# Three background chains in a row instead of overlapping, earlier weight preparation, and a one-pass spread of the softmax maximum

## The chip, the cores and the metric

The kernel runs on one core of one Trainium2 chip. The metric is the device time of one launch in microseconds (us). Five engines work side by side, each with its own queue of instructions that it executes in order: TensorE (PE in the profile, its weight loads PEld), VectorE (DVE), ScalarE (ACT), GpSimd (POOL) and SyncE (SP, which here issues all DMAs).

## The reference

The input `x` has 8 batches of 64 tokens with 512 channels, the context has 8 batches of 1601 rows with 512 channels. Six residual blocks follow one another:

```python
x = x + xattn(layernorm(x), ctx, Wq, bq, Wkv, bkv, Wo, bo)   # 32 query heads, 8 key/value heads of 128
x = x + mamba(layernorm(x), ...)                             # projection, conv of 4, silu, selective scan, gate
x = x + ffn(layernorm(x), ternarize(weight), bias)
x = x + softmax(layernorm(x) @ ctx.T) @ ctx
x = x + causal_attention(layernorm(x), wq, wk, wv, wo)       # 32 heads of 16
x = x + octonion_ffn(layernorm(x), w_gate, w_up, w_down)     # ternary weights
```

The scan of the second block keeps, for each of 1024 channels, 16 states: `state = state * exp(dt * A) + dt * u * B`, `y = sum(state * C)`, over the 64 tokens of a batch.

## The kernel before

**Main work.** `x_all` (L527) computes the first block. It runs over 64 units, one for each batch b and key/value head i (unit 8b + i). A unit has six steps: keys (`x_k`, L354), values (`x_v`, L319), scores (`x_s`, L369) with a copy to SBUF and a running maximum, then for the unit before it `x_max`, `x_spread`, `x_exp`, `x_av` and `x_o`, and `x_wo` (L496) for the output projection of two batches. Keys, values and scores are computed in three float32r products (high and low parts), the rest in float32.

**The maximum.** `x_max` (L397) transposes the maxima into PSUM (L403), and DVE reduces them to one negated column `mc` (L405). `x_spread` (L408) spreads that column over all partitions with a matmul against the identity, `m_ps` (L412), once for each half of 128 queries; `x_exp` adds it to the scores (L426) before the exponential. Column and identity are float32. TensorE executes a float32 matmul here as two instructions, a float32r matmul or a transpose as one.

**Background work.** Two kinds of generators run beside the units. `prep` (L616) splits and ternarizes the weights of the later blocks and writes them to DRAM. `chain` (L779) takes a group of two batches through blocks two to six: `mamba`, `ffn`, `xattn1`, `attn1`, `ffn1`. There are four groups, so chains 0 to 3. Chains 0, 1 and 2 are started when the main work has finished batches 1, 3 and 5. Chain 3 starts after the last unit, in another form ("tail"), with more PSUM and SBUF buffers.

**Pace.** Each `yield` of a generator reports a cost. `run` (L1303) keeps a clock `now` that advances by one for each batch of main work (236 cost units), and `advance` (L1331) draws from each background generator until it has got its share: its total cost (`CHAIN_COST` 377, `PREP_COST` 168) times the elapsed part of its span (`SPAN`, and `PREP_END` for `prep`). With the spans of before, 3.1 batches for chains 0 and 1, chain 1 starts before chain 0 has ended, and chain 2 before chain 1.

**Order.** That pace gives only the order in which the program is written. A scheduler then fixes each engine's order. The instructions of background work on DVE, ACT and POOL are pinned (class `Late`, L55): they keep the written order among themselves on their engine, so what is written later can't overtake. In the profile they all have line L65, whatever they do; on TensorE the background work has its own lines.

**The scan.** `scan` (L895) is called 32 times for each of chains 0 to 2: four blocks of states (`sh`), eight channel groups (`c`) each. A call does four exponentials on ACT into a tile `da`, a memset and a product `h = B * du` on POOL (called M1 in what follows), the scan on DVE, a product with C on POOL (M2), a reduction on DVE, and an addition into `u` on POOL (for `sh` 0 instead another product on POOL at its start and an operation on DVE). `da` and `h` are two of the five buffers named `a2`; the tile `bc` with B and C has one buffer and is loaded anew for each `sh`. The four steps of a call are followed by a `yield 1` each, so 128 of a chain's 377 cost units belong to the scan. After the scans come the gates (16 matmuls at L819 for each half), and `mamba_out` with 24 matmuls at L774, L776 and L777.

**The end.** When the last unit is done, `run` closes the pools of the main work and of `mamba`'s tiles (`ca`), and chain 3 gets its buffers from that memory:

```python
if last:
    self.pinning = False
    xctx.close()
    actx.close()
    self.pc = ctx.enter_context(tc.tile_pool(name="pt", bufs=3, space=PSUM))
    self.ca = self.cp = self.tp = ctx.enter_context(tc.tile_pool(name="tp", bufs=2))
```

Of the kernel before, what the change touches and what calls it, by code (L numbers as in the profile page):

```python
# [9 lines left out]
FR = mybir.dt.float32r  # L10
# [6 lines left out]
P = 128  # L17
# [61 lines left out]
class Kernel:  # L79
# [67 lines left out]
    def consts(self):  # L147
        nc, i = self.nc, self.i
        c = self.ctx.enter_context(self.tc.tile_pool(name="const", bufs=1))
        self.c = c  # L150
        self.ident = c.tile([P, P], FP, name="ident")
        make_identity(nc, self.ident)
        self.eps5 = c.tile([P, 1], FP, name="eps5")
        nc.gpsimd.memset(self.eps5, 1e-5)
        self.ones = c.tile([P, P], FP, name="ones")
        nc.gpsimd.memset(self.ones, 1.0)
        self.eps6 = c.tile([P, 1], FP, name="eps6")
        nc.gpsimd.memset(self.eps6, 1e-6)

        def ld(name, shape):  # L160
            t = c.tile(shape, FP, name="c_" + name)
            nc.sync.dma_start(out=t, in_=i[name])
            return t

        self.bq = ld("bq", [P, 32])
        self.bk = ld("bk", [P, NKV])
        self.bv = ld("bv", [P, NKV])
# [229 lines left out]
    def x_max(self, b, i):  # L397

        nc = self.nc
        m = self.mf.pop((b, i))  # L400
        ps = self.px.tile([P, 2, 256], FP, name=self.nm("m_ps"), tag="m", bufs=MB)
        for h in range(2):
            nc.tensor.transpose(ps[:, 0, h * P : (h + 1) * P], m[:, 0, h * P : (h + 1) * P], self.ident)  # L403
        col = self.sb("mc", [P, 2], pool=self.xp, bufs=2)
        nc.vector.tensor_reduce(col, ps[:, 0].rearrange("p (h k) -> p h k", k=P), AX.X, ALU.max, negate=True)  # L405
        self.mm[(b, i)] = (ps, col)

    def x_spread(self, b, i):  # L408

        ps, col = self.mm[(b, i)]  # L410
        for h in range(2):
            self.nc.tensor.matmul(  # L412
                ps[:, 1, h * P : (h + 1) * P], lhsT=col[:, h : h + 1].to_broadcast([P, P]), rhs=self.ident, start=True, stop=True
            )

    def x_exp(self, b, i, n):
# [390 lines left out]
    def mamba(self, gi, x, xo):  # L807
        nc, i = self.nc, self.i
# [36 lines left out]
        ps = self.acc()  # L845
# [20 lines left out]
        for h in range(2):  # L866
            ps = self.acc()
# [27 lines left out]
        def scan(c, sh, bc):  # L895
            da = self.sb(self.td, [P, HS, 2, T])
            for s in range(HS):
                k = sh * HS + s
                nc.scalar.activation(da[:, s], dt[:, c], AF.Exp, scale=self.A[:, c, k : k + 1])
            nc.gpsimd.memset(da[:, :, :, 0:1], 0.0)  # L900
            du = dus[:, c]
            if sh == 0:
                nc.gpsimd.tensor_tensor(du, dt[:, c], u[:, c], ALU.mult)
            h = self.sb(self.ts, [P, HS, 2, T])
            nc.gpsimd.tensor_tensor(h, bc[:, 0], du[:, None].to_broadcast([P, HS, 2, T]), ALU.mult)

            yield 1
            hf, df = h.rearrange("p s b t -> p (s b t)"), da.rearrange("p s b t -> p (s b t)")
            nc.vector.tensor_tensor_scan(hf, df, hf, 0.0, ALU.mult, ALU.add)
            yield 1  # L910
            nc.gpsimd.tensor_tensor(h, h, bc[:, 1], ALU.mult)
            yield 1
            y = da[:, 0]
            nc.vector.tensor_reduce(y.rearrange("p b t -> p (b t)"), h.rearrange("p s b t -> p (b t) s"), AX.X, ALU.add)
            if sh == 0:
                nc.vector.scalar_tensor_tensor(u[:, c], u[:, c], self.Dp[:, c : c + 1], y, ALU.mult, ALU.add)
            else:
                nc.gpsimd.tensor_tensor(u[:, c], u[:, c], y, ALU.add)
            yield 1

        wps = None
        if tail:
# [18 lines left out]
            for c in range(NCH):  # L941
                du = self.sb("du", [P, 2, T])
                nc.gpsimd.tensor_tensor(du, dt[:, c], u[:, c], ALU.mult)
                for k0 in range(0, NST, CS):
# [6 lines left out]
                    h = h8[:, o : o + CS]  # L951
# [14 lines left out]
        else:  # L966
            for sh in range(nh):
                bc = bcast(sh)
                for c in range(NCH):
                    yield from scan(c, sh, bc)  # L970
# [332 lines left out]
    def run(self):  # L1303
        nc, tc, ctx = self.nc, self.tc, self.ctx
        nc.scalar.preload_act_table_set("natural_log_exp_and_others")
        self.setup(bufs=BUFS, accb=2, hs=4, tail=False, ahead=1, **TAGS)
        self.pc = ctx.enter_context(tc.tile_pool(name="pc", bufs=2, space=PSUM))
        xctx = ctx.enter_context(ExitStack())
        self.px = xctx.enter_context(tc.tile_pool(name="px", bufs=2, space=PSUM))
        self.consts()  # L1310
        self.scratch()
        self.xw = ctx.enter_context(tc.tile_pool(name="xw", bufs=2))
        self.xp = xctx.enter_context(tc.tile_pool(name="xp", bufs=2))
        qctx = ctx.enter_context(ExitStack())
        self.q_ln(qctx.enter_context(tc.tile_pool(name="qp", bufs=2, side="right")))
        B = self.B
        sizes = GROUPS.get(B) or [1] * B
        groups, k = [], 0
        for m in sizes:
            groups.append(list(range(k, k + m)))  # L1320
            k += m
        self.place = {b: (k * T, len(g) * T) for g in groups for k, b in enumerate(g)}
        side, self.tp = [], None

        def start(gen, now, cost, end):
            env = {k: getattr(self, k) for k in ENV}
            if not self.tail:
                env["nc"] = Side(self, PINNED)
            side.append({"gen": gen, "cost": cost, "got": 0.0, "t0": now, "end": end, "env": env})

        def advance(now):  # L1331
            base = {k: getattr(self, k, None) for k in ENV}
            for c in list(side):
                self.setup(**c["env"])
                goal = c["cost"] * min(1.0, (now - c["t0"]) / max(c["end"] - c["t0"], 1e-9))
                if now >= c["end"]:
                    goal = 1e9
                while c["got"] < goal:
                    try:
                        c["got"] += next(c["gen"])  # L1340
                    except StopIteration:
                        if PRINT_COST:
                            print("side", c["got"])
                        side.remove(c)
                        break
            self.setup(**base)

        gi, now, xdone = 0, 0.0, 0.0
        for cost, fin in self.x_all(list(range(B))):
            xdone += cost  # L1350
            if not self.flush:
                advance(xdone / X_COST)
            if fin == 0:
                qctx.close()
                self.cp = ctx.enter_context(tc.tile_pool(name="cp", bufs=2, side="right"))
                actx = ctx.enter_context(ExitStack())
                self.ca = actx.enter_context(tc.tile_pool(name="ca", bufs=2, side="right"))
                start(self.prep(), xdone / X_COST, PREP_COST, PREP_END)
            if fin is not None and gi < len(groups) and groups[gi][-1] == fin:
                g = groups[gi]  # L1360
                now = xdone / X_COST
                last = gi == len(groups) - 1
# [4 lines that stand above are left out]
                    self.pc = ctx.enter_context(tc.tile_pool(name="pt", bufs=3, space=PSUM))  # L1367
                    self.ca = self.cp = self.tp = ctx.enter_context(tc.tile_pool(name="tp", bufs=2))
                    self.setup(bufs=BUFS_TAIL, accb=6, hs=8, tail=True, ahead=2, **TAGS_TAIL)
                start(self.chain(gi, g), now, CHAIN_COST, now + SPAN[gi])  # L1370
                if last:
                    side.insert(0, side.pop())
                gi += 1
        while side:
            now += 0.01
            advance(now)
# [3 lines left out]
TAGS_TAIL = {"tw": "w2", "ts": "s4", "td": "s4", "tc4": "s4", "tk": "kb", "t4": "s4", "tl": "s4", "tn": "w2", "tv": "s4"}  # L1380
ENV = ("nc", "cp", "ca", "pc", "bufs", "accb", "hs", "tail", "ahead", *TAGS)
GROUPS = {8: [2, 2, 2, 2], 2: [2]}
SPAN = [3.1,3.1,2.6,0.2]
PREP_END = 2.8
MAMBA_TAGS = ("a2", "lv", "bc", "xpad", "sm")
FFN_TAIL = (("l", 0), ("l", 1), ("a", 0), ("l", 2), ("a", 1), ("d", 0), ("a", 2), ("d", 1), ("d", 2))
REST = {"w2":8,"b4":3}
# [3 lines left out]
PREP_COST = 168.0  # L1391
PRINT_COST = False
CHAIN_COST = 377.0


@with_exitstack
# [106 lines left out]
```

## Time and profile before

| | |
|---|---|
| median of 3 runs | 2708.26 us (2706.93 to 2709.93) |
| the profiled execution | 2710.54 us, span 2708.8 us |
| PE busy | 2569.9 us (95% of the span) |
| DVE, ACT, POOL busy | 1670.9, 1354.6, 1253.5 us |
| mean granted TensorE clock | 0.977 |
| first scores of unit 0, of unit 63 | 51.7 us, 2346.7 us |
| last matmul of the main work (L521) | ends at 2404.3 us |
| last matmul of chain 2's `mamba` (L777) | at 2393.8 us |
| first matmul of chain 3 (L727 into `acc` from `a`) | at 2408.4 us |

The time of a run is that of the whole launch; the span runs from the first to the last instruction of the profiled execution. A line of a group has the source line, the engine, the operation, what it writes and reads, the shapes and the count, then the merged busy time in us, the mean of one in ns, and the idle time of the engine just before them with what ended it. A line of a timeline has the start and the duration in us, and in brackets the idle time before it.

### The profile page before, as it was taken

What the parts mean: (1) busy time and instruction counts of PE and PEld (TensorE: products, weight loads), DVE (VectorE), ACT (ScalarE), POOL (GpSimd) and SP (SyncE); (2) the same over time, 40 slices, a digit from 0 to 9 for tenths busy, and PEclk for the clock granted to TensorE, in tenths of its full rate; (3) what the DMA queues carried; (4) which work ended last, traced back from release to release, by engine and by line L of the source; (5) the groups of instructions that cost most, each with busy time, mean ns of one, the idle gap of its engine ahead of it and who ended that gap; (6) DMA issues with size and microseconds to landing.
All of it is one profiled execution on the core that took longest, in us unless ns stands there. A gap on an engine that the chain in (4) does not pass through costs nothing.

```text
span 2708.8 us, 43887 instructions
## 1 busy us (share of the span) xinstructions
PE 2569.9 (95%) x16288; PEld 2274.8 (84%) x16288; DVE 1670.9 (62%) x2723; ACT 1354.6 (50%) x3128; POOL 1253.5 (46%) x1243
## 2 busy tenths in 40 slices
PE   7999999999999899999999999999999999977787
PEld 6999999889899799978988988988898888964545
DVE  4444345577687865545577676554657777668744
ACT  4444554444566554544455545544546545446443
POOL 3212434464589864422358457521239556405410
PEclk9999999999999999999999999999999999987898
DMA  9544446665666235655234543665343454476764
GB/s 309 153 141 155 137 144 227 200 209 179 212 215 204 71 117 164 210 185 172 88 110 135 157 148 101 206 197 173 101 133 91 137 162 151 141 236 216 233 234 174
DMA packets 302934, 455.59 MB, mean 168 GB/s; under 512 B 80248, under 2 KB 179576, under 8 KB 298240
## 3 DMA queue, kind: packets, MB, share of 16 engines
q1 hardware_dynamic: 302720, 452.79, 52.2%
q8 instruction: 128, 2.10, 0.3%
q14 instruction: 86, 0.70, 0.1%
HBM read 380.23 MB, written 72.48 MB: 167 GB/s over the span
## 4 chain that ended last, share of the span: by engine, by line
PE 67%; DVE 10%; POOL 9%; DMA 7%; issue 4%; ACT 3%; SPq 0%; POOLq 0%; DVEq 0%; ACTq 0%
PE v_ps L334 15%; PE k_ps L363 15%; PE o_ps L464 10%; PE s_ps L385 8%; POOL a L65 4%; DVE a L65 3%; PE w_ps L521 3%; PE acc L274 3%; PE acc L819 2%; PE acc L1095 2%; POOL ss L452 2%; PE acc L1039 2%; PE acc L774 1%; PE acc L777 1%; DMA d_wo<-b 1%
## 5 line engine op out<-in xcount | busy, mean ns | idle before, releaser
L363 PE MATMUL k_ps<-cxb,wk 128*128 128x384 f32 x2304 | 469.9, 347 | 32.1 <-DVE mx L392 16.8
L334 PE MATMUL v_ps<-wv,cxb 128*128 128x256 f32 x3456 | 471.0, 283 | 1.4 <-DVE mx L392 1.2
L334 PEld LDWEIGHTS v_ps<-wv,cxb 128*128 128x128 f32 x3456 | 439.2, 189 | 22.0 <-issue 14.0
L363 PEld LDWEIGHTS k_ps<-cxb,wk 128*128 128x128 f32 x2304 | 405.2, 191 | 50.2 <-DVE mx L392 19.8
L464 PE MATMUL o_ps<-S,v 128*128 128x256 f32 (+1 forms) x1664 | 413.3, 381 | 6.0 <-DVE rw L479 3.9
L385 PE MATMUL s_ps<-q,kt 128*128 128x256 f32 (+1 forms) x2496 | 413.7, 299 | 5.2 <-DVE kt L109 3.1
L388 ACT COPY S<-s_ps 128x512 f32<-128x512 f32 (+1 forms) x448 | 242.4, 553 | 250.0 <-PE s_ps L385 246.9
L385 PEld LDWEIGHTS s_ps<-q,kt 128*128 128x128 f32 (+1 forms) x2496 | 342.1, 185 | 28.0 <-issue 6.9
L452 POOL TENSOR_TENSOR ss<-ss,S 128x512 f32<-128x512 f32 x254 | 353.7, 1392 | 14.6 <-ACT S L427 1.5
L429 POOL TENSOR_TENSOR ss<-S,S 128x512 f32<-128x512 f32 x64 | 85.0, 1328 | 586.9 <-ACT S L427 586.6
L392 DVE TENSOR_TENSOR mx<-s_ps,mx 128x512 f32<-128x512 f32 x256 | 175.4, 685 | 289.5 <-ACT S L388 288.8
L464 PEld LDWEIGHTS o_ps<-S,v 128*128 128x128 f32 (+1 forms) x1664 | 299.5, 190 | 45.0 <-issue 5.7
L108 ACT ACTIVATE kt<-k_ps,c_bk 128x384 fp32r<-128x384 f32 (+1 forms) x256 | 152.0, 594 | 240.7 <-PE k_ps L363 239.6
L426 DVE TENSOR_TENSOR S<-S,m_ps 128x512 f32<-128x512 f32 (+1 forms) x448 | 257.3, 641 | 24.4 <-PE m_ps L412 23.9
L427 ACT ACTIVATE S<-S 128x512 f32<-128x512 f32 (+1 forms) x448 | 247.4, 599 | 44.4 <-DVE S L426 43.8
L109 DVE SCALAR_TENSOR_TENSOR kt<-k_ps,c_bk,kt 128x384 fp32r<-128x384 f32 (+1 forms) x256 | 161.0, 629 | 170.9 <-ACT kt L108 169.4
L337 ACT COPY v<-v_ps 128x256 f32<-128x256 f32 (+1 forms) x416 | 152.7, 369 | 198.1 <-PE v_ps L334 195.7
L334 PE MATMUL v_ps<-wv,cxt 128*128 128x256 f32 (+1 forms) x1536 | 213.2, 286 | 2.7 <-DVE kt L109 1.6
L334 PEld LDWEIGHTS v_ps<-wv,cxt 128*128 128x128 f32 (+1 forms) x1536 | 195.3, 176 | 15.5 <-issue 6.5
L65 DVE TENSOR_TENSOR_SCAN a<-a,a 128x512 f32<-128x512 f32 x96 | 156.1, 1629 | 65.4 <-POOL a L65 65.4
L363 PE MATMUL k_ps<-cxt,wk 128*128 128x450 f32 x768 | 181.1, 378 | 0.9 <-DVE mx L392 0.8
L65 ACT ACTIVATE a<-lv,c_A_log 128x128 f32<-128x128 f32 x384 | 123.0, 394 | 105.3 <-DVE a L65 103.8
(358 smaller groups left out, 3971.3 us busy)
## 6 DMA issues: line engine op xcount, KB each, us to landing
wo<-d_wo SPq DMA_DIRECT2D x96, 512.0 KB, 5.0
wk<-d_wk SPq DMA_DIRECT2D x63, 512.0 KB, 3.8
wv<-d_wv SPq DMA_DIRECT2D x31, 1024.0 KB, 5.6
cst<-in_ctxT_dram SPq DMA_DIRECT2D x96, 192.0 KB, 3.1
b<-in_ctxN_dram SPq DMA_DIRECT2D x36, 512.0 KB, 3.9
d_q<-q_t SPq DMA_DIRECT2D x32, 512.0 KB, 4.4
q<-d_q SPq DMA_DIRECT2D x64, 256.0 KB, 3.5
d_wo<-b SPq DMA_DIRECT2D x32, 512.0 KB, 3.1
```

Of the source, the lines that this page charges most:

```text
L65: return lambda *a, **k: self.tc.keep_in_program_order(f(*a, **k))
L109: eng.scalar_tensor_tensor(lo, src, bias, hi.bitcast(FP), ALU.add, ALU.subtract)
L334: nc.tensor.matmul(ps[:r], lhsT=cx[:, a, c, o : o + r], rhs=w[:, m, c, :], start=k == 0, stop=k == 11)
L337: nc.scalar.copy(vt[:r], ps[:r])
L363: nc.tensor.matmul(ps[:, :wd], lhsT=w[:, a, c, :], rhs=cx[:, m, c, :], start=k == 0, stop=k == 11)
L385: nc.tensor.matmul(sp[:r, gi, :], lhsT=kt[:, a, o : o + r], rhs=q[:, m, :], start=k == 0, stop=k == 2)
L388: nc.scalar.copy(s[:r, :n], sp[:r, :n])
L392: nc.vector.tensor_tensor(mx, sp, S[0] if len(S) == 1 else mx, ALU.max)
L426: nc.vector.tensor_tensor(sv, sv, ps[:r, 1:2].to_broadcast([r, w, 256]), ALU.add)
L427: nc.scalar.activation(sv, sv, AF.Exp, scale=ISC)
L452: nc.gpsimd.tensor_tensor(ss, ss, S[n], ALU.add)
L464: nc.tensor.matmul(ps[:, 0], lhsT=self.v[(b, j, t)][:r, hc : hc + P], rhs=S[t // 2][:r, t % 2], start=t == 0, stop=t == NT - 1)
```

## The change

Four things are changed. The spans of chains 0 and 1 are 2.05 batches instead of 3.1, so that the spans of chains 0, 1 and 2 no longer overlap: each ends about where the next chain is started. In these two chains the steps of the scan report a cost of 2 instead of 1 (`SCAN_COST`), and the total is 505 instead of 377, so that 256 of 505 belong to the scan. `PREP_END` is 2.3 instead of 2.8. And the column `mc` is a float32r tile, which is multiplied with a float32r copy of the identity, `ident_r`, that ACT makes at the start. Lines below the first edit move by two.

```diff
         nc.gpsimd.memset(self.ones, 1.0)
+        self.ident_r = c.tile([P, P], FR, name="ident_r")
+        nc.scalar.copy(self.ident_r, self.ident)
...
-        col = self.sb("mc", [P, 2], pool=self.xp, bufs=2)
+        col = self.sb("mc", [P, 2], FR, pool=self.xp, bufs=2)
         nc.vector.tensor_reduce(col, ps[:, 0].rearrange("p (h k) -> p h k", k=P), AX.X, ALU.max, negate=True)
...
-                ps[:, 1, h * P : (h + 1) * P], lhsT=col[:, h : h + 1].to_broadcast([P, P]), rhs=self.ident, start=True, stop=True
+                ps[:, 1, h * P : (h + 1) * P], lhsT=col[:, h : h + 1].to_broadcast([P, P]), rhs=self.ident_r, start=True, stop=True
...
-            yield 1
+            yield SCAN_COST[gi]
             hf, df = h.rearrange("p s b t -> p (s b t)"), da.rearrange("p s b t -> p (s b t)")
             nc.vector.tensor_tensor_scan(hf, df, hf, 0.0, ALU.mult, ALU.add)
-            yield 1
+            yield SCAN_COST[gi]
             nc.gpsimd.tensor_tensor(h, h, bc[:, 1], ALU.mult)
-            yield 1
+            yield SCAN_COST[gi]
...
-            yield 1
+            yield SCAN_COST[gi]
...
-                start(self.chain(gi, g), now, CHAIN_COST, now + SPAN[gi])
+                start(self.chain(gi, g), now, CHAIN_COST + 128 * (SCAN_COST[gi] - 1), now + SPAN[gi])
...
-SPAN = [3.1,3.1,2.6,0.2]
-PREP_END = 2.8
+SPAN = [2.05, 2.05, 2.6, 0.2]
+PREP_END = 2.3
...
+SCAN_COST = [2, 2, 1, 1]
```

## The prediction

> **What bounds the kernel now.** First the page's slices of the span, then stretches of it, then its end, then one scan.
>
> ```profile
> PE   7999999999999899999999999999999999977787
> ...
> POOL 3212434464589864422358457521239556405410
> PEclk9999999999999999999999999999999999987898
> ```
>
> TensorE is full until slice 35, then for five slices it is not, and its clock falls. So there are two parts: main work, paced by PE, up to 2404 us, and a tail of 300 us that hangs on chains of dependent steps. Three stretches say the same in us (busy time and count of PE, PEld, DVE, ACT, POOL; then granted clock, DMA share, GB/s):
>
> ```profile
> 340.90:634.40 293.50, 289.75 (x1870) 266.56 (x1870) 176.40 (x318) 140.00 (x295) 143.94 (x135) 1.00 0.60 194
> ...
> 2072.10:2346.70 274.60, 259.36 (x1676) 236.83 (x1674) 204.12 (x287) 141.48 (x349) 166.15 (x178) 0.99 0.40 127
> 2408.40:2708.80 300.40, 241.97 (x1321) 155.51 (x1319) 191.97 (x360) 139.60 (x369) 87.80 (x92) 0.86 0.67 225
> ```
>
> Without scans (first row) PE idles 3.8 us in 293; beside chain 2's scans (second row) 15.2 us in 275; in the tail 58 us in 300. The timeline of PE at the seam:
>
> ```profile
> 2393.81 0.39 PE L777 MATMUL acc<-w,a 128*128 128x512 f32 x1
> ...
> 2397.61 3.32 PE L521 MATMUL w_ps<-wo,ot 128*128 128x512 f32 x9 [2.98 <-ACT ot L108]
> ...
> 2403.33 0.96 PE L521 MATMUL w_ps<-wo,ot 128*128 128x512 f32 x3 [0.38 <-DMA wo<-d_wo]
> ...
> 2408.41 0.60 PE L727 MATMUL acc<-ident,a 128*128 128x128 f32 x4
> ```
>
> Chain 2's `mamba` ends (L777) just before the main work does (L521); then chain 3 begins (L727) and takes 300.4 us to the end of the span. Chain 3's buffers lie in the memory of the main work and of `mamba`, so it needs both to be done.
>
> **What the change does to the order.** The changed program's order on each engine is fixed when it is built, and can be read without a time in it. Before, chain 0's matmuls stand in units 17 to 43, chain 1's in 33 to 60, and all of chain 2's `mamba` from unit 50 to the seam. Changed, chain 0 stands in 19 to 41, chain 1 in 41 to 62, and chain 2 begins in unit 62. The spans say 2.05 batches, 16 units, but a chain gets through in 21, and being pinned, a chain written wholly after another can't start before it is done. The lag of five units each adds up. Chain 2's 32 scans stand on DVE behind the last addition of the main work (L524), all of them; on PE its gates and `mamba_out` stand behind the last L521, and chain 3's first L727 behind those. So a stage that lay beside matmuls now lies alone between the main work and the tail, with PE empty. That is the forecast; its size follows. The scan's halved share does not show: chain 0's scans stood in units 20 to 28 and now stand in 22 to 28.
>
> **Part 1: the end of the main work (before 2404.3 us).**
> The spread:
>
> ```profile
> L412 PE MATMUL m_ps<-ident,mc 128*128 128x128 f32 x256 | 41.1, 283 | 5.9 <-DVE mc L405 5.8
> L403 PE MATMUL m_ps<-ident,mx 128*128 128x128 f32 x128 | 25.4, 275 | 0.4 <-DVE mx L395 0.4
> ```
>
> 128 matmuls of two instructions become 128 of one. The nearest row with one instruction of the same shape is L403: 41.1 - 25.4 = 15.7 us off PE. No row has float32r at 128 columns; the bounds are 0 (one instruction as slow as two) and 23.5 us (31.6 us, the sum of the steps from end to end in L412, less 128 times 0.063, from the 0.117 of the values' float32r at 256 columns less 128 columns at 0.42 ns). I take 15.7, since L412 comes, like L403, in pairs with other work around them.
> The skill has a lower price: "TensorE: Matmul & The Clock Gate", section "Back-to-back issue gap", gives 81 ns for weight load and matmul of 128 columns in a long stream; 128 of them would be 10.4 us, and the total would be 15 us lower. No run here shows such a stream, and these come in pairs.
>
> PE work that moves behind the main work: 64 instructions of chain 2's gates at 0.112 us and 24 of `mamba_out` at 0.23 us (distance of ends in a row of such instructions), 12.7 us, with smaller ones 13. Idle time that goes with chain 2's scans: 15.2 us, less 3.5 that such a stretch has without scans, plus 2.7 of clock (0.01 of 274.6) = 14.4 us, between 0 and 23. Against it, in units 22, 24, 44 and 48 the DVE work in the new order exceeds PE's (36.2 against 31.2 us, 34.6 against 31.7, 40.3 against 34.0, 39.4 against 34.4), 19 us at most; but the units after them have room (17 to 25 us of DVE in 27 to 30), and fewer units have two chains, which returns 0 to 10 us. I set these two against each other, at 0.
> Main work ends at 2404.3 - 15.7 - 13 - 14.4 = 2361 us, bounds 2345 to 2380.
>
> Nothing is counted for: `prep`, whose operations are the same and stand about one unit earlier, in a stretch where PE is full (3.8 us idle in the first row; without that cover 4 us either way); `ident_r`, 0.3 us on ACT, which waits until 8.5 us for its first data anyway; `mc` in float32r, the same reduction; 184 more semaphore waits on four engines, 17 to 51 ns each, under 1 us on any path.
>
> **Part 2: chain 2 alone, with all that it issues.**
> From the last L521, near which the `dt` matmuls stand, to the first M1. POOL's order puts both halves' softplus before it: 12.4 us for the first half (0.9 matmuls, 1.5 + 1.3 on ACT, 4.7 for four POOL operations of 1.08 and 1.29, 2.8 on DVE, hops), 4.7 more on POOL for the second: 18 us, bounds 13 and 21 (chain 3, from its `dt` matmuls at 2444.4 to its first scan at 2465.7).
> One scan, on POOL, where nothing was in its way:
>
> ```profile
> 2263.68 0.11 POOL L65 MEMSET a<- 128x8 f32 x1
> 2263.74 1.29 POOL L65 TENSOR_TENSOR a<-bc,lv 128x512 f32<-128x512 f32 x1
> 2266.36 1.29 POOL L65 TENSOR_TENSOR a<-a,bc 128x512 f32<-128x512 f32 x1 [1.34 <-DVE a L65]
> 2268.85 0.46 POOL L65 TENSOR_TENSOR lv<-lv,a 128x128 f32<-128x128 f32 x1 [1.20 <-DVE a L65]
> 2269.25 0.11 POOL L65 MEMSET a<- 128x8 f32 x1
> ```
>
> M1, a wait for the scan, M2, a wait for the reduction, the addition, the next memset: 5.6 us a round, POOL idle for 2.5 of it. The new order has it so in four of eight scans of each later block; the others stand in pairs (M1, M1, M2, M2, two additions), 7.6 us a pair by the same durations. So a block of eight is 4 x 5.6 + 2 x 7.6 = 37.6 us, three are 112.8. The first block has no addition on POOL: 3.9 us from M1 to the end of M2, in four of eight 0.57 more, 33.5 us. Between blocks `bc` is loaded: from M2 to the next M1 4.0 us (8 of 9 such gaps lay between 3.9 and 4.6), 2.3 more than in a round: 6.9. Together 153 us. Bounds: 131 if all of the later scans ran as pairs; 200, four times the fastest block beside main work (47.0 us, 1604.0 to 1650.9) and three gaps. I take 153, because rows without a rival on DVE are what is left here.
> The last reduction and addition: 1.6 us. Then two halves of silu, four `mamba_out` each, the second half with four loads of `W_in` into `a2`: 5 + 5 us for the first; 9 (loads and projections, partly beside it), 6 and 5 for the second, with what is exposed: 28 us. Upper bound 50, the second half before (2344 to 2394, beside the main work); lower 20. To chain 3's L727: 4.8 us (the sum `xr`, then as from L524 at 2404.3 before).
> Sum: 2361 + 18 + 153 + 1.6 + 28 + 4.8 = 2566 us. SP's queue: chain 3's loads now stand behind chain 2's; no main load is left to wait.
>
> **Part 3: the tail.** From there both versions are in the same state, chain 3 at its start, chain 2 at `ffn`: 300.4 us, give or take 10, since chain 2 was 8 us ahead. Span 2566 + 300.4 = 2867 us. The profiled run took 1.7 us more than its span, and the median is 2.3 us under that run: 2866 us, 158 us (5.8%) slower.
> The same page, section "Why this matters for your kernels", speaks against the change: gaps of over 3 us put TensorE back to half clock. Before, the tail has a clock of 0.86 against 1.00, so the row agrees; after an idle stage the rule would add 1.7 us (half of 3.4), which I leave out.
>
> **Rivals.**
> A. Faster: chain 3 is not held by chain 2's `mamba`, and the scans run beside the tail, where POOL idles 213 us of 300. For it: POOL's row. Against: the seam before, and the order, where L727 stands behind the last L777. Time 2361 + 4.8 + 300.4 = 2666 us plus contention, up to 2700. It decides if the stage between takes under 42 us (2708.3 - 2666) instead of 205. Chance 0.04.
> B. The scans keep the pace that they had beside main work: 47 us a block, 2866 + 47 = 2913 us. For: the fastest blocks there. Against: DVE and ACT are free here. 0.13.
> C. PE becomes late in the main work, the DVE-dense units costing their 19 us, or nothing saved at L412: 2882 to 2885 us, inside the forecast.
> D. Most waits overlap, pairs throughout, short gates, a main work 15 us faster: 2810 to 2835 us. 0.13.
> E. The change doesn't do what it says. It does not quite: the chains follow one another, but at 21 units each, not 16; that is the forecast's ground, not a rival.
>
> **How the numbers follow.** Forecast with C, 2835 to 2900 us: 0.70. D 0.13, B 0.13, A 0.04. The range takes in D's upper and B's lower part: 2815 to 2915 us. The measurement can't tell 0.2% (5.4 us) from no change; faster by more 0.03, within 0.01 (both A's), slower 0.96.
>
> **What would show it.** Right: a stretch of about 200 us near 2360 to 2560 with PE almost empty and POOL over half busy; chain 3's L727 near 2566 us, about 300 us before the end; L412 with 128 instructions and about 25 us. Wrong: scans of chain 2 beside the units' matmuls; L727 near 2365 us; a tail much longer or shorter than 300 us.

## The result and the profile after

The changed kernel takes 2931.0 us (median of 4, 2928.2 to 2936.6), the kernel before 2707.6 us on the same chip: a ratio of 1.0829, 95% interval 1.0808 to 1.0851. The forecast was 2866 us in a range of 2815 to 2915. The direction and the cause were right; 223 us were lost where 158 were forecast, and the time lies 16 us above the range. The profiled execution of after took 2928.2 us with a span of 2926.4 us. Medians and ratios, here and in the experiments (e1 to e16), leave out four executions in a slow state, which took over 4200 us.

The slices of the span on the page of after (one digit for 73 us, tenths):

```profile
PE   7999999999998999999999998999999940056798
...
POOL 2222445665597624223422787224232236505420
PEclk9999999999999999999999999999999965567899
```

PE stays full up to slice 32 and then has a hole in slices 33 to 36: 4, 0, 0, 5. POOL works on in the first three (3, 6, 5), and the granted clock falls to 5. That is the stage that the forecast put there. Its parts, as stretches of the span of after (from and to, length, then busy time and count of PE, PEld, DVE, ACT, POOL; granted clock, DMA share, GB/s):

```profile
1600.00:2000.00 400.00, 375.35 (x2418) 340.63 (x2417) 266.44 (x386) 200.52 (x492) 221.68 (x229) 0.98 0.39 125
2000.00:2378.60 378.60, 370.89 (x2362) 327.78 (x2360) 185.65 (x358) 171.91 (x374) 105.14 (x103) 0.98 0.47 152
2378.60:2398.90 20.30, 2.07 (x8) 1.77 (x8) 8.52 (x14) 5.76 (x14) 9.85 (x11) 0.50 0.00 0
2398.90:2556.80 157.90, 1.54 (x7) 1.57 (x8) 83.08 (x73) 39.36 (x124) 100.40 (x125) 0.50 0.04 12
2556.80:2609.90 53.10, 24.55 (x83) 17.30 (x81) 12.63 (x32) 8.41 (x26) 1.93 (x7) 0.60 0.36 121
2609.90:2926.40 316.50, 249.15 (x1332) 157.35 (x1332) 194.55 (x362) 140.11 (x370) 87.87 (x92) 0.85 0.65 217
```

The rows are, from above: two stretches of the main work, from its last matmul to chain 2's first M1, the 32 scans, the gates and `mamba_out` up to chain 3's first transpose (L729), and the tail. Against the forecast:

| step | forecast | measured | miss |
|---|---|---|---|
| main work ends (last L523) | 2361 | 2378.6 | +17.6 |
| to the first M1 | 18 | 20.3 | +2.3 |
| 32 scans | 153 | 157.9 | +4.9 |
| last M2 to L729 | 34.4 | 53.1 | +18.7 |
| tail | 300.4 | 316.5 | +16.1 |

So what was mis-sized is the main work, the gates and the tail, by some 17 us each; the long item, the scans, was right within 5.

The timeline of PE in after shows the hole and what ends it:

```profile
2376.91 1.65 PE L523 MATMUL w_ps<-wo,ot 128*128 128x512 f32 x3
2378.88 2.07 PE L874 MATMUL acc<-sm,a 32*128 32x128 f32 x8 [0.31 <-DMA a<-in_W_dtT_dram]
2555.26 2.04 PE L821 MATMUL acc<-a,a 128*128 128x128 f32 x8 [174.31 <-DMA a<-in_W_inT_dram]
2560.03 4.99 PE L821 MATMUL acc<-a,a 128*128 128x128 f32 x24 [2.73 <-DMA a<-in_W_inT_dram]
2571.21 0.80 PE L776 MATMUL acc<-w,a 128*128 128x512 f32 x1 [6.19 <-ACT a L65]
...
2575.07 0.80 PE L778 MATMUL acc<-w,a 128*128 128x512 f32 x1 [1.78 <-DMA w<-d_wout]
...
2593.75 0.79 PE L776 MATMUL acc<-w,a 128*128 128x512 f32 x1 [6.10 <-ACT a L65]
...
2605.19 0.63 PE L779 MATMUL acc<-w,a 128*128 128x512 f32 x1
2609.94 1.09 PE L729 MATMUL acc<-ident,a 128*128 128x128 f32 x4 [4.12 <-DVE a L144]
```

After `dt` (L874) PE waits 174.31 us for a load of `W_in`: the load goes into an `a2` buffer, and the scans hold those. Then come the projections of the gates, a silu (6.19 us of waiting), four `mamba_out` with waits for `d_wout`, a second silu and four more.

### The profile page after: what moved, and what is told of

It reads as the page before. It is cut to its first block, busy times and chain, and to the rows that moved or that the text cites. A ratio compares the mean times of both kernels' runs of the same rounds, so it can differ in the third digit from the quotient of the medians.

```text
span 2926.4 us, 43818 instructions
## 1 busy us (share of the span) xinstructions
PE 2576.8 (88%) x16160; PEld 2266.8 (77%) x16160; DVE 1670.5 (57%) x2723; ACT 1356.1 (46%) x3129; POOL 1228.5 (42%) x1243
## 4 chain that ended last, share of the span: by engine, by line
PE 60%; POOL 12%; DVE 11%; DMA 9%; issue 5%; ACT 3%; SPq 0%; POOLq 0%; DVEq 0%; ACTq 0%
PE v_ps L336 14%; PE k_ps L365 13%; PE o_ps L466 8%; PE s_ps L387 7%; POOL a L65 6%; DVE a L65 5%; PE acc L276 3%; POOL ss L454 2%; PE w_ps L523 2%; PE acc L1097 2%; PE acc L776 2%; PE acc L821 2%; PE acc L1041 1%; PE acc L779 1%; DMA cst<-in_ctxT_dram 1%
## 5 line engine op out<-in xcount | busy, mean ns | idle before, releaser
L454 POOL TENSOR_TENSOR ss<-ss,S 128x512 f32<-128x512 f32 x254 | 345.3, 1359 | 14.1 <-ACT S L429 0.3
L428 DVE TENSOR_TENSOR S<-S,m_ps 128x512 f32<-128x512 f32 (+1 forms) x448 | 257.2, 640 | 27.8 <-PE m_ps L414 27.5
L821 PE MATMUL acc<-a,a 128*128 128x128 f32 x384 | 55.0, 294 | 181.9 <-DMA a<-in_W_inT_dram 181.9
```

The costliest lines, as they stand in the source:

```text
L428: nc.vector.tensor_tensor(sv, sv, ps[:r, 1:2].to_broadcast([r, w, 256]), ALU.add)
L454: nc.gpsimd.tensor_tensor(ss, ss, S[n], ALU.add)
```

## The experiments

Two theories stood against each other. The first is the forecast's: the spans of chains 0 and 1 push chain 2's `mamba` behind the main work, and that is the whole loss. The second: the loss, or a large part of it, comes from the other edits (the faster spread, the earlier preparation, the scan's weights) or from denser scans beside the units. All times below are in us. "Seam" is from the last main matmul to chain 3's first transpose, "tail" from there to the end; ratios are to the kernel before on the same chip. Stage times are read from one profiled execution of each kernel, while the launches of after alone lie 8 us apart; a difference of a few us between two stages says little by itself.

| kernel | main work ends | first M1 | last M2 | seam | tail | median | ratio (95%) |
|---|---|---|---|---|---|---|---|
| before | 2404.3 | 2034.9 | 2326.4 | 4.1 | 300.4 | 2707.6 | 1 |
| after | 2378.6 | 2398.9 | 2556.8 | 231.3 | 316.5 | 2931.0 | 1.0829 (1.0808 to 1.0851) |
| e1 spread alone | 2394.9 | 2048.4 | 2350.0 | 25.7 | 310.4 | 2729.8 | 1.0061 (1.0044 to 1.0079) |
| e2 preparation alone | 2404.6 | 2036.0 | 2327.4 | 4.1 | 293.3 | 2704.0 | 0.9972 (0.9960 to 0.9984) |
| e3 scan's weights alone | 2376.8 | 1998.8 | 2369.2 | 46.9 | 304.8 | 2730.5 | 1.0059 (1.0041 to 1.0077) |
| e4 spans alone | 2380.6 | 2382.9 | 2540.7 | 215.3 | 308.1 | 2909.1 | 1.0718 (1.0699 to 1.0737) |
| e5 chain 1 at 3.1 | 2405.0 | 2082.1 | 2443.6 | 92.8 | 308.8 | 2805.3 | 1.0343 (1.0327 to 1.0360) |
| e6 chain 0 at 3.1 | 2369.5 | 2351.5 | 2512.5 | 197.6 | 315.5 | 2880.2 | 1.0621 (1.0605 to 1.0637) |
| e7 not pinned | 2420.8 | 2324.1 | 2483.4 | 118.1 | 318.0 | 2859.6 | 1.0551 (1.0531 to 1.0570) |
| e8 weights in `w2` | 2392.1 | 2376.5 | 2537.1 | 195.8 | 309.7 | 2899.4 | 1.0688 (1.0672 to 1.0704) |
| e9 float32 spread | 2389.0 | 2409.9 | 2567.9 | 231.3 | 308.8 | 2936.0 | 1.0838 (1.0821 to 1.0854) |
| e10 `W_out` in `b2` | 2375.3 | 2377.5 | 2535.9 | 209.1 | 307.7 | 2896.0 | 1.0692 (1.0677 to 1.0706) |
| e13 no scans in chain 1 | 2363.2 | 2364.7 | 2523.1 | 215.2 | 307.6 | 2889.0 | 1.0650 (1.0634 to 1.0666) |
| e14 scan's weights at 1 | 2382.0 | 2402.4 | 2560.4 | 231.9 | 317.6 | 2928.3 | 1.0798 (1.0782 to 1.0815) |

### Which edit costs the time: e1 to e4

Each of the four edits alone, in the kernel before.

```diff
e1:  mc and ident_r in float32r, nothing else
e2: -PREP_END = 2.8
    +PREP_END = 2.3
e3: -            yield 1
    +            yield SCAN_COST[gi]        # SCAN_COST = [2, 2, 1, 1], total cost as in the change
e4: -SPAN = [3.1,3.1,2.6,0.2]
    +SPAN = [2.05, 2.05, 2.6, 0.2]
```

> The kernel before with the float32r spread alone (mc and ident_r). Theory (the whole loss comes from the spans of the chains): L412's 256 instructions become 128 and 15.7 us leave PE's path in the main work, chain 2's scans stay beside units 54 to 63, so about 2692 us, 0.994 of before, with L412 near 25 us. Rival 1 (the spread's time was never on the path, or the rearranged order gives it back at the seam, where chain 2's mamba now ends after the main work): 2705 to 2712 us. Rival 2 (the spread itself costs time in the changed kernel): over 2715 us.

> The kernel before with the end of the weights' preparation at 2.3 batches in place of 2.8, nothing else. Theory: prep lies where PE is full, so no more than 5 us either way, 2703 to 2713 us. Rival (the earlier loads and DVE work of prep delay the units beside it): 10 us or more above 2708.

> The kernel before with the weights of a scan's steps in the pacing (2, 2, 1, 1) alone, spans and the rest as before, the spread in float32. Theory: chains still overlap, chain 2's scans end in unit 63 where they ended in 62, so 2705 to 2725 us. Rival (the halved share of the scans is what costs, because it puts scans closer together in DVE-dense units): 2760 us or more.

> The kernel before with the spans 2.05 and 2.05 in place of 3.1 and 3.1, nothing else. Theory: all of the loss is here; chain 2's 32 scans stand in unit 63 behind the main work, and without the faster spread the main work ends some 15 us later than in the changed kernel: 2926 + 1.7 + 15 = about 2943 us, 2925 to 2955. Rival (the loss needs the spread, the preparation or the scan's share too): under 2850 us.

The spans alone lose 7.2% of the 8.3%, and the stage is there again: 157.8 us of scans with PE empty. So the loss is the spans'. The number was missed: 2909 us where 2925 to 2955 were expected, because chain 2's softplus stood ahead of the last main matmul, so that the first M1 follows that matmul after 2.3 us and not 20.3, because the tail was 8.4 us shorter than in after, and because the main work, without the faster spread, ended only 2.0 us later than in after and not 15.

The other three edits are worth 0.6% or less each. But e1 and e3 lose where their main work gained: in both the main work ends earlier (by 9.4 and 27.5 us), and chain 2's `mamba` ends later. The seam of e1 as a stretch, from the last main matmul to L729:

```profile
2394.90:2420.60 25.70, 8.79 (x29) 4.94 (x28) 8.27 (x23) 4.03 (x13) 1.48 (x5) 0.60 0.37 124
```

Before, the seam was 4.1 us, and main work and chain 2 ended together. Here 20 of chain 2's matmuls, 28 instructions in the trace, stand on PE behind the last main matmul (56 instructions in e3, 96 in after), and what the spread saves comes back as a wait with PE 34% busy at a clock of 0.60. The time is rival 2's, over 2715 us, but the way is rival 1's: the gain is given back at the seam, and 10 us more in the tail. e2 lies where it was expected, e3 6 us above.

### Which span, and what holds the chain: e5, e6, e7

```diff
e5: -SPAN = [2.05, 2.05, 2.6, 0.2]
    +SPAN = [2.05, 3.1, 2.6, 0.2]
e6: -SPAN = [2.05, 2.05, 2.6, 0.2]
    +SPAN = [3.1, 2.05, 2.6, 0.2]
e7: -PINNED = ("vector", "scalar", "gpsimd")
    +PINNED = ()
```

> The changed kernel with chain 1's span back at 3.1, chain 0's left at 2.05. In the built order chain 1 keeps its place (scans in units 43 to 48), but chain 2 is interleaved with its end and its scans stand in units 54 to 63 again. Theory (the loss is chain 2 standing alone behind the main work): 2690 to 2730 us, no idle stage. Rival (the loss comes from denser chains, the dense units 44 to 48 or the spread): over 2800 us.

> The changed kernel with chain 0's span back at 3.1, chain 1's left at 2.05. Chain 2's scans stand in unit 63 as in the changed kernel, so theory: 2915 to 2945 us, with about 158 us of scans and 230 us of idle stage again. Rival (two short spans are needed to push chain 2 out, or the dense units count for much): under 2880 us.

> The changed kernel without the pinned order on DVE, ACT and POOL. The prediction said that the pinned order keeps a chain from starting before the one written ahead of it is done. If that alone held chain 2, its scans would move back to unit 48 and the time to about 2700 us. The built order speaks against it: even unpinned chain 1's first transpose stands behind chain 0's last matmul, chain 2's scans begin in unit 61 and end in unit 63. Rival to the pins: the two PSUM buffers of acc, taken in turn in the order in which the chains are written, which hold a chain's first transpose until the chain ahead has used its last. By that, scans start about 2 units earlier and only some 16 of 32 stand behind the main work: 2830 to 2880 us.

Chain 1's span is the one that decides: with it at 3.1 the loss falls from 8.3 to 3.4%, with chain 0's at 3.1 only to 6.2%. The sizes were missed in both. e6 lies on the bound of its rival (2880 us), since the scans begin 18 us ahead of the end of the main work, which itself ends 9 us earlier than in after. e5 lies in the range of its rival, over 2800 us. Chain 2's scans do begin beside the units (at 2082 us), but they don't get done: from the first M1 to the last M2 they take 361.5 us, where they took 291.5 before. The stretches from the end of the main work to L729 in e5:

```profile
2405.00:2443.60 38.60, 1.68 (x8) 1.71 (x8) 19.64 (x16) 7.62 (x24) 24.90 (x30) 0.50 0.03 10
2443.60:2497.80 54.20, 24.64 (x82) 17.47 (x81) 12.61 (x32) 8.41 (x26) 1.93 (x6) 0.59 0.36 120
```

The last block of scans and the whole of the gates still stand alone, 92.8 us. So most of what e5 loses is again the seam, 88.7 us more than before of 97.8 us more span; why chain 2's scans took longer beside the units was not tried. The unit in which a stage begins says little; what stands behind the last main matmul says what it costs.

In e7 the pins are gone, and chain 2's scans begin only about 75 us earlier than in after, at 2324 us: the pins were not all that held it. In e7, too, PE runs a chain's first transpose directly behind the last matmul of the chain ahead: 1472.5 us behind 1472.2 for chain 1, 2229.7 behind 2229.4 for chain 2. The two PSUM buffers of `acc`, into which both write, are handed out in the order in which the chains are written, so a chain that is written wholly after another has to wait for it there too. That these buffers are what holds it is read from the order and was not tried by itself. The main work ended 42 us later in e7 than in after, with the scans beside its end.

### The gates: e8 and e10

```diff
e8:  -TAGS = {"tw": "a2", ...
     +TAGS = {"tw": "w2", ...
e10: -... c == NCH - 1, tg=self.t4)                                   # w2, three buffers
     +... c == NCH - 1, tg=self.t4 if self.tail else "b2")            # five buffers
```

> The changed kernel with mamba's weight tiles (W_in, W_x, W_dt) in the w2 buffers in place of a2. In the changed kernel PE's first gate projection (L821) waited 174.3 us for a load into an a2 buffer that the scans held, and the stretch from the last M2 to L729 took 53.1 us where 34.4 were forecast. Theory (that wait is the term that failed): the projections run during the scans and the stretch falls to about 35 us, total 2908 to 2918 us. Rival (the stretch is long because of the low clock, the weight loads and the silus): 45 us or more in that stretch and 2922 to 2935 us.

> The changed kernel with the W_out loads of mamba_out in the b2 buffers (five) in place of w2 (three). In the changed kernel the two sets of four mamba_out took 13.3 and 12.1 us, PE waiting 1.7 to 2.8 us before three of each four for a load from d_wout; the forecast had 5 us a set. Theory (three buffers for two loads each time make that wait): sets of 7 to 9 us, the stretch from the last M2 to L729 about 44 us where it was 53.1, total 2920 to 2924 us if the scans begin where they did. Rival (the loads are limited by their own queue or latency, not by buffers): sets of 12 us again, stretch 50 us or more.

In e8 the first projections run during the scans, and the first silu begins with the end of the last M2. Still the stretch to L729 takes 50.8 us where it took 53.1: the second half's projections now stand in the same three `w2` buffers behind the loads of `W_out`, and PE gets through them only from 2556.4 to 2564.8, up to 21.6 us after the first `mamba_out`. The rival was right about the stretch: moving the wait to another buffer didn't remove it. Both missed the total, 2899 us. (The span fell by 28.8 us for other reasons: the scans began 22.4 us earlier, ahead of the end of the main work, and the tail was 6.8 us shorter.)

In e10 the second set of four `mamba_out`, from the timeline of PE:

```profile
2572.53 0.79 PE L776 MATMUL acc<-b,a 128*128 128x512 f32 x1 [6.09 <-ACT a L65]
...
2576.43 0.79 PE L778 MATMUL acc<-b,a 128*128 128x512 f32 x1 [0.55 <-DMA b<-d_wout]
...
2579.02 0.80 PE L778 MATMUL acc<-b,a 128*128 128x512 f32 x1 [0.94 <-DMA b<-d_wout]
2579.61 0.63 PE L779 MATMUL acc<-b,a 128*128 128x512 f32 x1
```

It ends at 2580.2: 7.7 us, where after needed 12.1 (2593.75 to 2605.82). The first set took 7.7 where it took 13.3. So the theory holds for the sets: three buffers for two loads each cost some 5 us a set. The second set is the cleaner comparison; the first of after also has projections of the second half between its matmuls, and the first of e10 ran at a granted clock of 0.75 where all the others had 0.50. The stretch is 48.5 us and not 44, since the second half's projections, which had been hidden behind the slow first set, now stick out for 8 us; as a whole the buffers are worth 4.6 us. (The total, 2896 us, lies under the 2920 expected because the scans began 21.4 us earlier and the tail was 8.8 us shorter.)

### The main work: e9, e13, e14

```diff
e9:  float32 spread as before (mc, ident), the rest as changed
e13: -            nc.vector.tensor_tensor_scan(hf, df, hf, 0.0, ALU.mult, ALU.add)
     +            if gi != 1:
     +                nc.vector.tensor_tensor_scan(hf, df, hf, 0.0, ALU.mult, ALU.add)
e14: -SCAN_COST = [2, 2, 1, 1]
     +SCAN_COST = [1, 1, 1, 1]
```

> The changed kernel with the spread back in float32 (mc, ident), the rest as changed. Theory of the forecast (PE paces the main work, so the spread's 17 to 18 us of PE time come back in full): 2944 to 2952 us, last L523 near 2396 us from the start. Rival (in the changed order part of that time is filled by PE's waits for DVE and POOL, as the run with the spans alone hinted, where the main work ended at 2380.6 us with the spread in float32): within 5 us of the changed kernel's 2931, PE idle in the main work lower by over 10 us than its 79.

> The changed kernel with the 32 tensor_tensor_scan instructions of chain 1 left out (its memsets, multiplications and reductions stay), so that some 39 us less of DVE's work lies in units 43 to 49; its output is therefore not the reference's for chain 1. Theory (units 43 to 49 have more DVE work than PE work, and PE waits for it): PE idle between 1600 and 2000 us falls from 24.6 to 8 to 14 us, the main work ends 10 to 17 us earlier than in the changed kernel (2362 to 2369), total 2905 to 2920 us. Rival (the idle time comes from something else, the hand-offs of the chain or buffers): idle time over 20 us, main work ends within 5 us of 2378.6.

> The changed kernel with the weights of the scan's steps back at 1 for all chains. Its built order has chain 1's scans in units 43 to 48 as in the changed kernel, one unit more for the last ones, and after the main work exactly the same order of TensorE's instructions. Theory 1 (the tail's length is set by its written order): tail 315 to 318 us from L729 to the end, as in the changed kernel, not 308. Theory 2 (the pacing weights matter little once chains do not overlap): main work ends within 5 us of 2378.6, total 2922 to 2936 us. Rival to 1 (the tail varies from run to run): 308 us or less. Rival to 2: main work 8 us or more earlier, as in the run with the spans alone.

PE's busy time in the main work fell by 26.7 us from before to after (2326.2 to 2299.5), but its idle time did not: 78.1 and 79.1. Where it moved is seen in the stretches of before:

```profile
1600.00:2000.00 400.00, 389.02 (x2517) 346.54 (x2515) 234.21 (x392) 195.20 (x464) 166.53 (x170) 0.99 0.48 154
2000.00:2404.30 404.30, 382.59 (x2429) 346.06 (x2428) 278.02 (x417) 206.34 (x498) 225.05 (x232) 0.98 0.44 138
```

Idle time went from 11.0 to 24.6 us in the first and from 21.7 to 7.7 in the second. The gain in the second, where chain 2's scans were, is 14.0 us of idle time (forecast 11.7, and 2.7 of clock, which is 0.98 in both). The loss in the first, 13.6 us, lies beside chain 1's scans, which ran in units 37 to 46 and now run closer, in 44 to 50. Without chain 1's 32 scan instructions (e13) the same stretch:

```profile
1600.00:2000.00 400.00, 389.31 (x2554) 353.74 (x2555) 219.65 (x368) 212.82 (x518) 214.90 (x235) 0.99 0.44 136
```

It idles 10.7 us, as before, and the main work ends at 2363.2, 15.4 us earlier; over the whole main work PE's idle time fell by 7.4 us (79.1 to 71.7), and its busy time by 8.0, at a granted clock of 0.993 and not 0.990, which in 2380 us is worth some 8 us. (The total fell by more than expected, since the first M1 now follows 1.5 us and not 20.3 us behind the main work, and the tail is 8.9 us shorter.) The waits of PE in this stretch say how, first of after, then of e13, then the largest of before (engine and line, what it waited for, total in us, times, longest):

```profile
PE o_ps L466 <- DVE rw L481: 8.7, 1, 8.7
PE k_ps L365 <- DVE kt L109: 5.9, 3, 3.2
PE m_ps L414 <- DVE mc L407: 2.8, 3, 1.7
PE k_ps L365 <- DVE mx L394: 2.5, 3, 1.3
```

```profile
PE o_ps L466 <- DVE rw L481: 7.5, 1, 7.5
PE k_ps L365 <- DVE kt L109: 1.1, 2, 0.8
PE k_ps L365 <- DVE mx L394: 1.0, 1, 1.0
...
PE m_ps L414 <- DVE mc L407: 0.2, 1, 0.2
```

```profile
PE k_ps L363 <- DVE mx L392: 5.3, 3, 2.6
```

Without the scans the repeated waits for small steps of DVE (`kt`, `mc`, `mx`) fall from 11.2 to 2.3 us, so DVE's load does make PE wait. But that is not most of what the change added: before, the same three waits came to 9.0 us in this stretch. What before does not have there is the single wait of 8.7 us, and in e13 it stays, with 7.5. It lies in unit 46; from the timelines of DVE and PE in after:

```profile
1755.00 3.40 DVE L428 TENSOR_TENSOR S<-S,m_ps 128x512 f32<-128x512 f32 x6
...
1760.90 0.42 DVE L481 TENSOR_TENSOR rw<-o_ps,sl 128x256 f32<-128x256 f32 x1
...
1761.47 2.04 PE L466 MATMUL o_ps<-S,v 128*128 128x256 f32 x4 [8.66 <-DVE rw L481]
```

In this unit DVE has seven additions of the maximum (L428) ahead of the operations that empty `o_ps` (L478 to L481); in most units it has none there. `o_ps` has one buffer, so PE waits. After, e4, e5, e6, e8, e9, e10, e13 and e14 have this wait, 6.2 to 9.4 us; the other kernels have no wait of PE over 4 us between 1600 and 2000 us. So of the 13.6 us, 8.7 are this wait, which comes with the new order and not with the scan instructions, and about 5 are left for the denser scans. Why the order puts the additions first stays open. The pacing weights are not the cause: with them at 1 (e14) the main work ends at 2382.0, 3.4 us later.

The spread, undone in the changed kernel (e9), costs 10.4 us at the end of the main work, less than the theory's 17. The rival's reason is refuted: PE's idle time in the main work is not lower, but 81.5 us against 79.1. Its busy time is only 8.0 us higher (2307.5 against 2299.5), but e9 had a granted clock of 0.993 up to there and after 0.990, some 8 us in 2380. At the same clock the spread would be worth nearer to the theory (an estimate). The group of after has 17.7 us less than L412 before:

```profile
L414 PE MATMUL m_ps<-ident_r,mc 128*128 128x128 f32 x128 | 23.4, 265 | 4.5 <-DVE mc L407 4.4
```

In the whole launch little of it is left: 2936.0 against 2931.0 us, ratios of 1.0838 and 1.0829 with intervals that overlap, since e9's tail is 7.7 us shorter.

### The tail

In all kernels of the table the tail has the same work, chain 3 and the rest of chain 2 (before and e2 have done a few matmuls of it earlier, 1321 records instead of 1332), and yet it takes 293.3 to 318.0 us. What differs is the order in which the two chains stand on the engines. From L729 on, the order of PE's 1332 instructions in the trace is one and the same in e4, e5, e8, e9, e10 and e13, and their tails take 308.1, 308.8, 309.7, 308.8, 307.7 and 307.6 us. It is another one, the same in both, in after and e14. The orders of ACT and POOL agree in the same two groups. The tails of e14 and, below it, of e9 as stretches:

```profile
2613.90:2931.50 317.60, 246.86 (x1332) 156.19 (x1332) 194.57 (x362) 139.98 (x370) 87.82 (x92) 0.85 0.66 216
```

```profile
2620.30:2929.10 308.80, 245.66 (x1332) 152.96 (x1332) 197.71 (x362) 140.28 (x370) 87.36 (x92) 0.87 0.67 222
```

316.5 and 317.6 us with the one order, 307.6 to 309.7 with the other, whatever came ahead of the tail. So the tail's length goes with its written order, theory 1 of e14. This also sizes e2's gain: its main work ends where it did before, and all of its 7 us are in the tail, which has the same instructions on PE in before and e2, but not in the same order.

### Versions meant to be faster: e11, e12, e15, e16

All four have the float32r spread, the preparation at 2.3 and the scan's weights at 1, and differ in the spans of chains 0, 1, 2: 3.0, 3.0, 2.4 (e11); 3.0, 3.0, 2.2 (e12); 3.0, 3.1, 2.5 (e15); 3.1, 3.0, 2.3 (e16).

```diff
-SPAN = [2.05, 2.05, 2.6, 0.2]
+SPAN = [3.1, 3.0, 2.3, 0.2]        # e16
```

> A version meant to beat both: the kernel before with the float32r spread, the preparation to 2.3, and spans 3.0, 3.0 and 2.4, so that chain 2's mamba stands ahead of the last main matmul again (two side instructions behind it on PE, where the run with the spread alone had 20 and the changed kernel 60). Theory (the spread's gain was lost only because chain 2 ended after the main work): main work ends near 2390 us, L729 4 us behind it, tail 293 to 300, total 2685 to 2697 us. Rival (the gain is taken by DVE and POOL waits, PE idle in the main work over 90 us): 2700 to 2712 us.

> As the run before it, with chain 2's span 2.2 in place of 2.4: its scans stand about one unit earlier (blocks begin in units 53, 55, 58, 59). Theory: within 8 us of the run before it, since chain 2's mamba is ahead of the last main matmul in both. Rival (denser scans of chain 2 delay the units 54 to 62): 10 us or more slower than it, PE idle in the last 400 us of the main work over 30 us.

> The kernel before with the float32r spread, the preparation to 2.3 and spans 3.0, 3.1 and 2.5. Here all of chain 2's mamba and its ffn's first transposes stand ahead of the last main matmul, as they did before, and the order of the tail is nearer to before's than that of any version with the spread so far. Theory (the spread's gain is real, and the runs with it lost it through the seam and the tail's order): main work ends near 2395 us, L729 about 4 us later, tail 293 to 302 us, total 2690 to 2703 us. Rival (more idle time in the main work eats the gain): 2704 to 2720 us; a tail of over 310 us would show that the lead isn't what makes the tail short.

> As the run before it with spans 3.1, 3.0 and 2.3: chain 2's mamba ahead of the last main matmul too, chain 2's ffn ahead by as much, but the tail's order is less like before's. Theory: the lead sets the tail, 293 to 305 us, total 2690 to 2710 us. Rival (the order within the tail matters more than the lead): over 310 us of tail.

| kernel | main work ends | seam | tail | median | ratio (95%) |
|---|---|---|---|---|---|
| e11 | 2418.9 | 5.7 | 336.5 | 2763.4 | 1.0202 (1.0188 to 1.0216) |
| e12 | 2408.4 | 5.8 | 340.2 | 2754.3 | 1.0163 (1.0149 to 1.0177) |
| e15 | 2424.2 | 7.6 | 306.8 | 2741.4 | 1.0106 (1.0092 to 1.0120) |
| e16 | 2398.8 | 3.8 | 307.0 | 2712.6 | 1.0001 (0.9992 to 1.0010) |

None is faster. e11, e15 and e16 lie above what the theory gave, and e12 lies 9 us under e11, where at most 8 were expected. The seam is short in all, as meant, but the other two terms moved. PE idles more in the main work: up to 2360 us it is idle 93.4 us in e11, 84.5 in e12, 88.9 in e15 and 77.4 in e16, against 71.8 before; that takes a part of the spread's time in e16, while in e11, e12 and e15 the main work ends later than before. And the tails were rewritten again. In e15 and e16 chain 2's `ffn` begins ahead of the last main matmul, as it does before and in e2 (300.4 and 293.3 us), and yet their tails take 307: that lead is not what makes a tail short. What in an order costs the 8, 16 or 40 us stays open. The only version that beats both kernels is e2, the earlier end of the preparation alone: it is 0.28% faster than before (0.16 to 0.40).

## Why the prediction was wrong in size

**What held.** The hole, its place and its cause: chain 2's `mamba` pushed behind the main work by the spans. The reason given for it, the pins, is only a part: without them (e7) chain 2's scans began 75 us earlier, and the last 62.6 us of them still stood alone. The scans took 157.9 us where 153 were forecast, and the same order alone gave 157.7 to 158.4 us in five experiments. From a block's first M1 to the end of its last M2 it was 34.5 us for the first block (forecast 33.5) and 37.4 for each of the others; the forecast's 37.6 runs on to the next M1, and up to the end of M2 it is 35.9. The price of a pair was too low, 7.6 us where after has 8.6; a single round took 5.45 (5.6), and the gaps between blocks 3.6 to 3.9 us (4.0). Rival B, scans at the pace beside main work, is refuted, as is rival A. A stage in pairs throughout (D) exists in another order: without pins (e7) the last two blocks, partly or wholly alone, took 31.5 us each.

**The step that failed first: the DVE-dense units set at 0** (17.6 us at the end of the main work). The forecast listed units 22, 24, 44 and 48 with DVE work above PE's, 19 us at most, and set this against room in the units after them. They did not cancel: PE's idle time rose by 13.6 us between 1600 and 2000 us, beside chain 1's scans. 8.7 us of that is one wait in unit 46, which comes from the order of DVE's steps and not from a sum of work in a unit, and about 5 are the denser scans. In the sum, PE's idle time in the main work was to fall by 11.7 us and rose by 1.0: 12.7 us of the miss. The clock adds some 7 us: it was granted at 0.992 before and 0.990 after up to the end of the main work, a loss of some 4 us where 2.7 were to be gained. Executions differ by as much: ahead of 1600 us, where e13 does the same work as after, the clock costs 5 us more in after. The spread was sized well; its group fell by 17.7 us where 15.7 were counted, and this gives 2 us back.

**The second: the gates at 28 us** (18.7 us). From the last M2 of after, with the forecast's terms in brackets: 8.5 us (1.6) until the first half's silu, since its projections could not run during the scans; 5.9 (5) for that silu; 13.3 (5) for the first four `mamba_out`; 3.5 (7, with what was put as exposed) until the second silu; 5.8 (6); 12.1 (5) for the other four; 4.1 (4.8) to L729. Two terms failed. The two sets of four took 15.4 us more than their matmuls were priced at: 4.8 us of it is the clock, 0.50 in both sets, and the rest nearly all the loads through three buffers, for which e10 shows 5.6 and 4.4 us (the first with some of the clock in it). The first half's projections cost 6.9 us that the forecast did not have; half of that comes back, since the second half's were hidden behind the slow first set. The forecast had an upper bound from a measured row, 50 us, and took 28 from its own list of steps; the row was the better guide.

**The third: a tail in "the same state"** (16.1 us). It has the same work, but its order on PE is another one. Between identical orders tails agreed within 2.1 us, between different ones they lay up to 47 us apart (293.3 in e2, 340.2 in e12), so the 10 us that were allowed were too few.

**The two places of the Trainium skill.** "TensorE: Matmul & The Clock Gate", section "Back-to-back issue gap", gives 81 ns for weight load and matmul in a long stream; here 128 of them took 23.4 us merged, 183 ns each, so the row of the trace was nearer than the stream's figure. The section "Why this matters for your kernels" says that gaps of over 3 us put TensorE back to half clock. The rows agree: 0.50 granted from the end of the main work to the last M2, and 0.60 in the gates. But the price was not at the tail's start alone, where 1.7 us had been worked out: the `mamba_out` matmuls themselves ran at half clock, 0.43 us from end to end of 128x512 where the rows before had 0.23. For 24 of them this is 4.8 us, part of the two slow sets.

## What to carry to other kernels

When a side chain is squeezed into a shorter span, count the instructions that stand behind the last main one on each engine, and cost that stage with its loads and its buffers, not only with its arithmetic. Where a scheduler writes the order anew for every edit, a stage that the edit doesn't touch is not constant: allow for it what identical work has cost in different orders, here up to 47 us of 300. And a gain on the engine that paces the main work counts only if what ends beside it also ends earlier: the spread alone took 9.4 us off the main work and made the launch 0.6% longer.

## What the runs showed that was not expected

The tail's time repeats within 2.1 us (307.6 to 309.7) over six different kernels on four chips if its order is the same, and is 8.8 us longer in e14 than in e9, with the same instructions in another order and little more busy time on PE (245.7 us in e9, 246.9 in e14). One scan beside an idle TensorE costs 4.7 us in the pinned order (37.4 us for eight) and 3.9 in the unpinned one (31.5), with the same instructions: in the second, POOL's products of two scans stand next to each other throughout, at 8.2 us for two, in the first in four of eight, at 8.6 us for two and 5.45 for one alone.
